# A gated cross-attention kernel: order of the visits, place of a sigmoid, and the softmax's small steps

## The chip, the cores and the metric

The kernel runs on one core of a Trainium2 chip. The metric is the device time of one execution in microseconds (us), the median of several runs. All data is fp32. The engines of the core are TensorE (PE in the profile; its weight loads are listed apart as PEld), VectorE (DVE), ScalarE (ACT), GpSimd (POOL) and SyncE (SP), which issues most DMAs.

## The reference

```python
# x: 8 x 1024 x 1024, ctx: 8 x 64 x 512
memory_proj = einsum('bme,de->bmd', ctx, W_mem)            # W_mem 1024 x 512
scores = einsum('bnd,bmd->bnm', x, memory_proj) / sqrt(1024)
attn = softmax(scores, axis=-1)                             # over 64 rows of memory
memory_context = einsum('bnm,bmd->bnd', attn, memory_proj)
gate = sigmoid(einsum('bnf,df->bnd', concat([x, memory_context]), W_gate) + b_gate)
fused = x + gate * memory_context
out = fused * rsqrt(mean(fused**2) + 1e-6) * norm_w
```

The gate's second half is not computed from `memory_context`: the kernel multiplies `memory_proj` with that half of `W_gate` once, so that each row's gate gets `attn` times the result, as its context gets `attn` times `memory_proj`.

## The kernel before, in words

The 8192 rows of `x` are taken in 16 passes (`q`) of 512 rows, two passes per batch. In each pass the product of x (512 x 1024) with the first half of `W_gate` is made by a fast matrix multiplication on two levels: seven outer products (`ORDER` = 1, 6, 7, 5, 4, 2, 3, line 633), each of them seven inner products of 128 x 256 x 256, where the operands are sums and differences made beforehand by VectorE and GpSimd. Some outer products' results go into several blocks of the gate.

`outer_product(q, o)` (line 889) issues one outer product. Its inner products are, in order: R11 into the bank `af`, whose result ScalarE copies at once into `u` (L910, "the first copy"); one into the bank `b` (`kB`); one into the bank `c` (`kC`); two into the bank `ed`; and two more into `af`, the sixth and seventh. VectorE's additions `u<-u,kB`, `u<-u,kC` and `u<-u,ed` follow their products. `pre` (GpSimd), `fin_ed` and `fin_af` (VectorE) add the results to the gate's blocks (tiles `gate`); all of these show as L96, the helper `tt`, and all matmuls as L93, the helper `mm`.

Two outer products of a pass, o=5 and o=2, are "held": their banks `af` and `ed` are not read at the end but kept until the next outer product, o=4 or o=3. There, behind the third inner product, stand the "visits": `visit` (line 830) multiplies the 64 rows of memory of this batch with the attention weights of one row block of 128 rows and one half of the columns, once into a context bank `pc`, once, added, into the gate's bank (`af` or `ed`). There are four visits, two for the held block (`f`) and two for the block of this outer product (`o`), in the order o first row, f first, f second, o second. The held block's contexts go into the banks `b` and `c`, from which VectorE's additions of `kB` and `kC` read just before. Then come the held block's additions `fin_af` and `fin_ed` and its gating: `gate` (line 882) issues the sigmoid on ScalarE (L695) and puts the multiplication with the context (`gated`, line 689) into a later slot. The own block's second row is gated after the fifth inner product, its first row after the seventh.

Order on an engine is program order. The program is written by slots: every inner product of 128 x 256 is one slot, a pass has 49, and `at(slot, fn)` or `mid((q, o, part), fn)` puts a step ahead of that slot's product or beside the visits of an outer product. `plan(q)` (line 636) places a pass's steps. Those of the softmax: the scores of the next pass are made by TensorE behind the visits of o=3 (`scores`, line 400), in pass q from 1 on into the two banks `af` and `ed` that the held block has just left, in pass 0 into `b` and `c` at slot 7; `turn_scores` in slot 1 turns them and takes the maxima over 32 columns, `softmax_max` in slot 8 copies the maxima between halves of the partitions, `softmax_exp` in slot 9 takes the larger, scales it by -1/32 on ScalarE (L447), takes the exponentials with their sums (L450) and copies the sums across, `softmax_scale` in slot 15 adds and inverts the sums (L464) and scales (L466), `turn_attn` in slot 19 turns the result. `transpose_x` turns the next pass's rows in 32 x 32 blocks on VectorE (L353), in slots 20 to 38 and, for two of the eight pieces, beside the visits of o=3.

The last pass (q=15) has no next pass; its additions of the residual, its squares and its norm are placed one by one (`last_gated`, `last_root`, `last_norm`).

Of the kernel before, what the change touches and what calls it, by code (L numbers as in the profile page):

```python
# [9 lines left out]
AF = mybir.ActivationFunctionType  # L10
ALU = mybir.AluOpType
# [4 lines left out]
P = 128  # L16
# [4 lines left out]
def tile_gated_cross_attention_rmsnorm(  # L21
# [42 lines left out]
    nc = tc.nc  # L64
# [11 lines left out]
    SCALE = 1.0 / float(D) ** 0.5  # L76
    Q4 = D // 4
    B32 = 32
# [6 lines left out]
    small = ctx.enter_context(tc.tile_pool(name="small", bufs=1))  # L85
# [4 lines left out]
    pin = tc.keep_in_program_order  # L90

    def mm(o, lhsT, rhs, start, stop):
        pin(nc.tensor.matmul(o, lhsT, rhs, start=start, stop=stop, skip_group_check=True))  # L93

    def tt(eng, o, a, b, op):
        pin(eng.tensor_tensor(o, a, b, op))  # L96
# [4 lines left out]
    def t4k(pool, shape, tag, name):  # L101
        return pool.tile(shape, F32, tag=tag, name=name)
# [31 lines left out]
    for k in range(KD):  # L134
        t = t4k(*((gpool, [P, D], "gate") if k < 7 else (apool, [P, D], "s4")), f"w2_{k}")
# [42 lines left out]
    eps_sb = const.tile([P, 1], F32, name="eps_sb")  # L178
# [161 lines left out]
    sTs, attnTs, scs, mxs, dens, mps, mgs = {}, {}, {}, {}, {}, {}, {}  # L340
# [90 lines left out]
        mx = mxs[q] = t4k(small, [P, 2, 8], "mx", f"mx{q}")  # L431
        pin(nc.vector.tensor_reduce(mx[:, 0], sc, AX.X, ALU.max))

    def other_half(o, i):

        for g in range(4):
            pin(nc.scalar.copy(o[g * B32 : (g + 1) * B32], i[(g ^ 1) * B32 : ((g ^ 1) + 1) * B32]))

    def softmax_max(q):
        mx = mxs[q]  # L440
        other_half(mx[:, 1], mx[:, 0])

    def softmax_exp(q):
        sc, mx = scs[q], mxs.pop(q)
        den = dens[q] = t4k(small, [P, 2, 8], "den", f"den{q}")
        tt(nc.vector, mx[:, 0], mx[:, 0], mx[:, 1], ALU.max)
        pin(nc.scalar.activation(mx[:, 0], mx[:, 0], AF.Copy, scale=-SCALE))  # L447
        for n in range(8):
            pin(
                nc.scalar.activation(  # L450
                    sc[:, n],
                    sc[:, n],
                    AF.Exp,
                    bias=mx[:, 0, n : n + 1],
                    scale=SCALE,
                    accum_out=den[:, 0, n : n + 1],
                )
            )
        other_half(den[:, 1], den[:, 0])

    def softmax_scale(q):
        sc, den = scs[q], dens.pop(q)
        tt(nc.vector, den[:, 0], den[:, 0], den[:, 1], ALU.add)
        pin(nc.vector.reciprocal(den[:, 0], den[:, 0]))  # L464
        for n in range(8):
            pin(nc.scalar.activation(sc[:, n], sc[:, n], AF.Copy, scale=den[:, 0, n : n + 1]))  # L466

# [158 lines left out]
    def at(slot, fn, *args):  # L626
        due.setdefault(slot, []).append(lambda: fn(*args))

    def mid(key, fn, *args):
        beside.setdefault(key, []).append(lambda: fn(*args))  # L630
# [5 lines left out]
    def plan(q):  # L636
        t0 = SLOTS * q
        nxt = q + 1 < NQ
        for i, o in enumerate(ORDER):
            for part, t in ((0, 1), (1, 2)):  # L640
                if i + 1 < len(ORDER):
                    at(t0 + 7 * i + t, inner_s, q, ORDER[i + 1], part)
                elif nxt:
                    at(t0 + 7 * i + t, inner_s, q + 1, ORDER[0], part)
        if q == 0:
            at(t0 + 7, scores, q)
            at(t0 + 8, add_scores, q)
        at(t0 + (3 if q else 7), outer_s, q, 3)
        at(t0 + (11 if q else 22), outer_s, q, 4)
        when = (9, 10, 11, 16, 19, 23) if q == 0 else (1, 8, 9, 15, 19, 23)  # L650
        steps = turn_scores, softmax_max, softmax_exp, softmax_scale, turn_attn, attn_difference
        for t, fn in zip(when, steps):
            at(t0 + t, fn, q)
        if not nxt:
            at(t0 + 12, load_last)
            return
        at(t0 + 2, load_xq, q + 1)
        for i, t, half in (
            (20, 0, 0), (21, 1, 0), (23, 2, 0), (25, 3, 0), (37, 2, 1), (38, 3, 1)
        ):  # L660
            at(t0 + i, transpose_x, q + 1, t, half)
        mid((q, 3, 0), transpose_x, q + 1, 0, 1)
        mid((q, 3, 1), transpose_x, q + 1, 1, 1)
        mid((q, 3), scores, q + 1)
        at(t0 + 46, add_scores, q + 1)
        mid((q, 3), outer_s, q + 1, 1)
        mid((q, 3), outer_s, q + 1, 2)
        if (q + 1) % QPB == 0:
            at(t0 + 10, load_mp, (q + 1) // QPB)
            at(t0 + 49, load_mg, (q + 1) // QPB)  # L670
        if q == 0:
            at(t0 + 8, add_bias, mgs[0][M:P, :])
            at(t0 + 20, add_bias, mgd[1, M:, :])
# [8 lines left out]
    slot = 0  # L682
# [116 lines left out]
            )  # L799
        load(out[b, n0 : n0 + P, cols], g)  # L800

    def sqrt_table():

        t = t4k(small, [P, 1], "warm", "warm")
        pin(nc.scalar.activation(t, eps_sb, AF.Sqrt))  # L805

    def blocks(q, row, r, h):

        t = 2 * row + r
        if (q, t) not in O:  # L810
            O[q, t] = t4k(gpool, [P, D], "gate", f"gate{q}_{t}")
        return O[q, t].rearrange("p (n c) -> p n c", c=C)[:, 2 * h : 2 * h + 2]
# [17 lines left out]
    def visit(q, o, r, pc, k):  # L830

        row, h, g = EXT[o]
        at_, mg = attnTs[q], mgs[q // QPB]
        second = o in SECOND
        cols = slice(h * H, (h + 1) * H)
        for t in TOKENS:
            mm(pc[t, :], at_[0:M, 2 * row + r, t], mg[0:M, cols], True, True)
        if second and r == 0:
            for n, left in ((0, g + r), (1, NEG[o])):
                part = mg[M:P, h * H + n * C : h * H + (n + 1) * C]  # L840
                for t in TOKENS:
                    mm(k[t, n], at_[M:P, upper(left), t], part, False, True)
        else:
            whole = k.rearrange("p n c -> p (n c)")
            for t in TOKENS:
                mm(whole[t, :], at_[M:P, upper(g + r), t], mg[M:P, cols], second, True)
# [42 lines left out]
    def outer_product(q, o):  # L889
# [4 lines left out]
        nxt = q + 1 < NQ  # L894
        af = bank(f"af{sets}", [P, 2, C], f"af{q}_{o}")
# [24 lines left out]
        if second:  # L920
            f = SECOND[o]
            faf, fed, fu3, fu4 = held.pop((q, f))
            frow, fh, _ = EXT[f]
            fp = [bank(t, [P, H], f"pc{q}_{f}_{r}") for r, t in enumerate("bc")]
            pcs = [ps_ctx.tile([P, H], F32, tag="ctx", name=f"pc{q}_{o}_{r}") for r in range(2)]
            visit(q, o, 0, pcs[0], af)
            visit(q, f, 0, fp[0], faf)
            visit(q, f, 1, fp[1], fed)
            visit(q, o, 1, pcs[1], ed)
        for fn in beside.pop((q, o, 0), ()):  # L930
            fn()
# [24 lines left out]
        if second:  # L956
            row, h, _ = EXT[o]
# [5 lines left out]
        if not first:  # L963
            fin_af(q, o, af, u4)
        if second:
            if o == 4 and not nxt:
                at(slot + 1, gate, q, 2 * row, h, pcs[0], 1)
            else:
                gate(q, 2 * row, h, pcs[0], 1)
        if second and not nxt:  # L970
            c, d = 2 * row, 2 * row + 1
            if o == 3:
                sqrt_table()
            when = (3, 4, 4, None, 10, 11) if o == 4 else (0, 2, 2, 2, 3, 3)
            if o == 4:
                for h_ in range(2):
                    mid((q, 3, 0), last_weigh, c, h_)
            at(slot + when[0], last_root, d)
            at(slot + when[1], last_root, c)
            for w_, (t, h_) in zip(when[2:], ((d, 0), (d, 1), (c, 0), (c, 1))):  # L980
                if w_ is None:
                    mid((q, 3, 0), last_norm, t, h_)
                else:
                    at(slot + w_, last_norm, t, h_)
        elif second:

            c, d = 2 * row, 2 * row + 1
            for t in (d, c):
                at(slot + 5, residual, q, t)
            if row == 0:  # L990
                when = (22, 23, -1, None, 33, -2) if q + 2 < NQ else (17, 18, 20, 22, 24, -1)
            else:
                when = (17, 18, 22, 24, 29, 31)
            at(slot + when[0], square, q, c)
            at(slot + when[1], square, q, d)
            for w_, (t, h_) in zip(when[2:], ((c, 0), (c, 1), (d, 0), (d, 1))):
                if w_ is None:
                    mid((q + 1, 4), norm, q, t, h_)
                elif w_ < 0:
                    mid((q + 1, 4, 0) if w_ == -1 else (q + 1, 3), norm, q, t, h_)  # L1000
                else:
                    at(slot + w_, norm, q, t, h_)
# [6 lines left out]
    while due:  # L1009
        slot = min(due)  # L1010
# [27 lines left out]
```

## Time and profile before

| | before |
|---|---|
| median of 3 runs | 952.65 us (952.65 to 952.77) |
| profiled execution | 951.76 us, of which span 950.0 us |
| mean granted TensorE clock | 0.996 |
| TensorE busy | 937.4 us, 99% of the span |
| VectorE busy | 818.1 us, 86% |
| GpSimd busy | 727.4 us, 77% |
| ScalarE busy | 414.0 us, 44% |

The share of TensorE is close to the whole span, so a change counts where TensorE's stream has a gap, or behind its last product. Timelines give the start of a group of like instructions in us from the span's start, how long the group lasted, the engine, the line, the operation with the program's names (out<-in), the number of instructions, and, in brackets, how long the engine was idle before and what ended that. A matmul of 128 x 256 in fp32 shows as two records, so an inner product shows as x4. In the rows of weight loads and of matmuls an idle time is counted on the queue of that kind.

### The profile page before, as it was taken

Reading aid. Unit: us, or ns where it says so; the run is one execution under the profiler, and the core shown is the slowest. Engines: PE = TensorE matmul, PEld = TensorE weight load, DVE = VectorE, ACT = ScalarE, POOL = GpSimd, SP = SyncE. Lnnn points to the kernel's source line nnn. Section 1 sums busy time; section 2 is a strip of 40 time slices with the busy share of each in tenths; the row PEclk is TensorE's granted clock in tenths of the full one; section 3 lists DMA queues with packets and bytes.
Section 4 is the critical chain, followed back from the end, with each engine's and each line's share of the span. In section 5 each row is a group of like instructions: output and inputs, shape, how many; then the busy total and the mean of one; then the engine's idle time right before and its main releaser. Section 6 shows DMA issues by size and latency. Waiting matters only on the chain. (4 is left out here: it accounts for less than half of the span.)

```text
span 950.0 us, 15819 instructions
## 1 busy us (share of the span) xinstructions
PE 937.4 (99%) x5560; PEld 730.6 (77%) x5560; DVE 818.1 (86%) x1274; ACT 414.0 (44%) x1086; POOL 727.4 (77%) x812
## 2 busy tenths in 40 slices
PE   9999999999999999999999999999999999999995
PEld 8546778787877778787877778787877778687873
DVE  6989788888988888888988888888988888888877
ACT  3000436273544527263543627263543627263555
POOL 5998878688687878678686868778686868778684
PEclk9999999999999999999999999999999999999998
DMA  9956664481919365491918366390918466390632
GB/s 377 285 146 163 104 123 110 110 179 44 212 45 181 93 141 131 97 192 34 220 48 166 101 135 144 85 204 27 213 61 158 110 133 145 76 213 25 150 138 90
DMA packets 70928, 128.44 MB, mean 135 GB/s; under 512 B 12352, under 2 KB 49216, under 8 KB 70592
## 3 DMA queue, kind: packets, MB, share of 16 engines
q1 hardware_dynamic: 61664, 93.86, 37.5%
q0 software_dynamic: 9184, 33.56, 19.4%
q8 instruction: 45, 0.74, 0.3%
q14 instruction: 35, 0.29, 0.1%
HBM read 87.56 MB, written 41.68 MB: 136 GB/s over the span
## 5 line engine op out<-in xcount | busy, mean ns | idle before, releaser
L96 POOL TENSOR_TENSOR gate<-gate,u 128x512 f32<-128x512 f32 (+1 forms) x224 | 237.6, 1072 | 162.2 <-DVE u L96 137.6
L695 ACT ACTIVATE gate<-gate 128x512 f32<-128x512 f32 x128 | 80.7, 630 | 263.8 <-DVE gate L96 263.8
L353 DVE STREAM_TRANSPOSE a<-xq 128x512 f32<-128x512 f32 x128 | 141.3, 1107 | 3.7 <-POOL it L96 3.7
L96 POOL TENSOR_TENSOR l<-a 128x256 f32<-128x256 f32 x128 | 116.4, 909 | 24.2 <-DVE a L96 22.7
L724 DVE SCALAR_TENSOR_TENSOR gate<-gate,ss,nw_sb 128x512 f32<-128x512 f32 x120 | 123.9, 1032 | 1.1
L93 PE MATMUL pc<-mg,attnT 64*64 64x512 f32 x512 | 117.0, 596 | 0.3 <-DVE u L96 0.3
L93 PE MATMUL ed<-it,l 128*128 128x256 f32 x448 | 115.0, 379 | 0.0
L93 PE MATMUL kB<-it,l 128*128 128x256 f32 x448 | 115.0, 379 | 0.0
L96 DVE TENSOR_TENSOR gate<-gate,pc 128x512 f32<-128x512 f32 x128 | 86.1, 682 | 31.7 <-ACT gate L695 31.7
L93 PE MATMUL af<-w,a 128*128 128x256 f32 x384 | 98.5, 379 | 0.0
L96 DVE TENSOR_TENSOR gate<-gate,af 128x512 f32<-128x512 f32 (+1 forms) x128 | 77.1, 612 | 20.0 <-PE af L93 11.6
L93 PEld LDWEIGHTS ed<-it,l 128*128 128x128 f32 x448 | 85.1, 190 | 11.6
L93 PEld LDWEIGHTS kB<-it,l 128*128 128x128 f32 x448 | 85.1, 190 | 11.6
L96 DVE TENSOR_TENSOR gate<-gate,ed 128x512 f32<-128x512 f32 x112 | 76.3, 681 | 17.1 <-POOL gate L96 13.5
L910 ACT COPY u<-af 128x256 f32<-128x256 f32 x112 | 40.9, 365 | 105.8 <-PE af L93 100.2
L93 PEld LDWEIGHTS af<-w,a 128*128 128x128 f32 x384 | 73.0, 190 | 10.4 <-issue 0.5
L96 POOL TENSOR_TENSOR l<-s 128x256 f32<-128x256 f32 x96 | 78.1, 813 | 3.0 <-PE af L93 3.0
L93 PEld LDWEIGHTS pc<-mg,attnT 64*64 64x64 f32 x512 | 33.0, 132 | 49.8 <-issue 44.8
L93 PE MATMUL ed<-it,a 128*128 128x256 f32 x256 | 67.4, 386 | 0.0
L96 DVE TENSOR_TENSOR u<-u,kB 128x256 f32<-128x256 f32 x112 | 45.6, 407 | 24.6 <-PE kB L93 21.0
L93 PE MATMUL af<-w,l 128*128 128x256 f32 x256 | 66.4, 382 | 0.1
L93 PE MATMUL af<-t,s 128*128 128x256 f32 x256 | 65.8, 379 | 0.0
(149 smaller groups left out, 2100.1 us busy)
## 6 DMA issues: line engine op xcount, KB each, us to landing
xq<-in_x SPq DMA_DIRECT2D x64, 512.0 KB, 10.3
gate<-in_x POOLq DMA_DIRECT2D x60, 512.0 KB, 8.1
out<-gate SPq DMA_DIRECT2D x60, 512.0 KB, 2.9
w<-in_w_gate_t SPq DMA_DIRECT2D x8, 512.0 KB, 10.2
w<-in_w_gate_t SPq DMA_DIRECT2D x2, 2048.0 KB, 16.9
mg<-mgd SPq DMA_DIRECT2D x16, 256.0 KB, 5.0
wm<-in_w_mem_t SPq DMA_DIRECT2D x4, 512.0 KB, 6.0
mpd<-mpT SPq DMA_DIRECT2D x4, 512.0 KB, 8.3
```

The costliest lines, as they stand in the source:

```text
L93: pin(nc.tensor.matmul(o, lhsT, rhs, start=start, stop=stop, skip_group_check=True))
L96: pin(eng.tensor_tensor(o, a, b, op))
L353: nc.vector.transpose(A[key][:, :, r * P : (r + 1) * P], chunks(xq[q][:, 4 * t : 4 * t + 4, :], KD)[:, half * KH : (half + 1) * KH],)
L695: pin(nc.scalar.activation(g, g, AF.Sigmoid))
L724: nc.vector.scalar_tensor_tensor(g[:, cols], g[:, cols], rstd[:, t % 2 : t % 2 + 1], nw_sb[:, cols], ALU.mult, ALU.mult,)
L910: pin(nc.scalar.copy(p1, af[:, 0]))
```

## The change

- Visits: the held block's two rows come first, then the two rows of the own block.
- Sigmoid: in all passes but the last, the gate of the own block's first row is issued one slot later for both o=4 and o=3: its sigmoid stands behind the next outer product's first copy, its multiplication another slot later. (In the last pass o=4 did so already, and o=3 stays as it is.)
- Maxima: the copies between halves multiply by -1/32 as they copy; VectorE then scales the own half and takes the smaller in one instruction, and ScalarE's scaling (L447) goes.
- exp's table: behind these copies, in slot 8, a one-element exp is issued, so that the table is loaded there.
- Sums: their addition and inversion become a step of their own, `softmax_sum`, in slot 13 (15 in pass 0); the scaling stays in slot 15 (16 in pass 0).
- `transpose_x` of piece (0, 1) goes from beside the visits of o=3 to slot 42, ahead of o=3's first product.

```diff
-    def other_half(o, i):
+    def other_half(o, i, scale):
         for g in range(4):
-            pin(nc.scalar.copy(o[g * B32 : (g + 1) * B32], i[(g ^ 1) * B32 : ((g ^ 1) + 1) * B32]))
+            pin(
+                nc.scalar.activation(
+                    o[g * B32 : (g + 1) * B32],
+                    i[(g ^ 1) * B32 : ((g ^ 1) + 1) * B32],
+                    AF.Copy,
+                    scale=scale,
+                )
+            )
+    def table(func):
+        t = t4k(small, [P, 1], "warm", "warm")
+        pin(nc.scalar.activation(t, eps_sb, func))
     def softmax_max(q):
         mx = mxs[q]
-        other_half(mx[:, 1], mx[:, 0])
+        other_half(mx[:, 1], mx[:, 0], -SCALE)
+        table(AF.Exp)
     def softmax_exp(q):
...
-        tt(nc.vector, mx[:, 0], mx[:, 0], mx[:, 1], ALU.max)
-        pin(nc.scalar.activation(mx[:, 0], mx[:, 0], AF.Copy, scale=-SCALE))
+        pin(nc.vector.scalar_tensor_tensor(mx[:, 0], mx[:, 0], -SCALE, mx[:, 1], ALU.mult, ALU.min))
...
-        other_half(den[:, 1], den[:, 0])
+        other_half(den[:, 1], den[:, 0], 1.0)
+    def softmax_sum(q):
+        den = dens[q]
+        tt(nc.vector, den[:, 0], den[:, 0], den[:, 1], ALU.add)
+        pin(nc.vector.reciprocal(den[:, 0], den[:, 0]))
     def softmax_scale(q):
         sc, den = scs[q], dens.pop(q)
-        tt(nc.vector, den[:, 0], den[:, 0], den[:, 1], ALU.add)
-        pin(nc.vector.reciprocal(den[:, 0], den[:, 0]))
...
-        when = (9, 10, 11, 16, 19, 23) if q == 0 else (1, 8, 9, 15, 19, 23)
-        steps = turn_scores, softmax_max, softmax_exp, softmax_scale, turn_attn, attn_difference
+        when = (9, 10, 11, 15, 16, 19, 23) if q == 0 else (1, 8, 9, 13, 15, 19, 23)
+        steps = (
+            turn_scores,
+            softmax_max,
+            softmax_exp,
+            softmax_sum,
+            softmax_scale,
+            turn_attn,
+            attn_difference,
+        )
...
-            (20, 0, 0), (21, 1, 0), (23, 2, 0), (25, 3, 0), (37, 2, 1), (38, 3, 1)
+            (20, 0, 0), (21, 1, 0), (23, 2, 0), (25, 3, 0), (37, 2, 1), (38, 3, 1), (42, 0, 1)
...
-        mid((q, 3, 0), transpose_x, q + 1, 0, 1)
         mid((q, 3, 1), transpose_x, q + 1, 1, 1)
...
-            visit(q, o, 0, pcs[0], af)
             visit(q, f, 0, fp[0], faf)
             visit(q, f, 1, fp[1], fed)
+            visit(q, o, 0, pcs[0], af)
             visit(q, o, 1, pcs[1], ed)
...
-            if o == 4 and not nxt:
+            if nxt:
+                at(slot + 1, gate, q, 2 * row, h, pcs[0], 1)
+            elif o == 4:
                 at(slot + 1, gate, q, 2 * row, h, pcs[0], 1)
             else:
                 gate(q, 2 * row, h, pcs[0], 1)
...
             if o == 3:
-                sqrt_table()
+                table(AF.Sqrt)
```

More of the change, by code (lines that the diff above doesn't have):

```diff
@@ L800, in last_norm @@
         load(out[b, n0 : n0 + P, cols], g)
-    def sqrt_table():
-        t = t4k(small, [P, 1], "warm", "warm")
-        pin(nc.scalar.activation(t, eps_sb, AF.Sqrt))
     def blocks(q, row, r, h):
```

## The prediction

> **What bounds the kernel now.** I read the page first, then the waits of TensorE's weight loads (PEld), because a matmul's end is modelled and its own waits hide stalls, and then timelines of pass 7 and of the last pass. Passes are the 16 groups of 512 rows; o=5, 4, 2, 3 are outer products; "visits" are the attention matmuls (`pc`, with `af` and `ed` beside them) ahead of the fourth product of o=4 and o=3.
>
> ```profile
> span 950.0 us, 15819 instructions
> PE 937.4 (99%) x5560; PEld 730.6 (77%) x5560; DVE 818.1 (86%) x1274; ACT 414.0 (44%) x1086; POOL 727.4 (77%) x812
> ```
>
> TensorE is the bound: it has work for 99% of the span. The changed lines add no matmul and take none away, so only three things can move the time: a stall of TensorE inside its stream, the tail behind its last product, and new stalls. Weight loads run ahead of matmuls, so their idle time shows where TensorE was held:
>
> ```profile
> PEld psT_af L93 <- DVE gate L96: 4.1, 15, 0.3
> PEld af L93 <- POOL l L96: 3.7, 10, 0.7
> PEld af L93 <- issue: 1.3, 4, 0.4
> ```
>
> Two places come back pass after pass: the scores (`psT`, 15 times) and a product into `af` (10 times). Pass 7 shows the second, VectorE, then ScalarE, then TensorE:
>
> ```profile
> 495.83 0.68 DVE L96 TENSOR_TENSOR gate<-gate,af 128x512 f32<-128x512 f32 x1
> 497.20 0.69 DVE L96 TENSOR_TENSOR gate<-gate,pc 128x512 f32<-128x512 f32 x1 [0.70 <-ACT gate L695]
> ```
> ```profile
> 496.54 0.63 ACT L695 ACTIVATE gate<-gate 128x512 f32<-128x512 f32 x1 [1.35 <-DVE gate L96]
> 497.08 0.35 ACT L910 COPY u<-af 128x256 f32<-128x256 f32 x1
> ```
> ```profile
> 495.70 1.03 PE L93 MATMUL ed<-it,a 128*128 128x256 f32 x4
> 496.57 1.03 PE L93 MATMUL ed<-it,l 128*128 128x256 f32 x4
> 497.58 1.10 PE L93 MATMUL af<-w,l 128*128 128x256 f32 x4
> ```
>
> Products follow each other at 0.87 (495.70 to 496.57); the sixth product of o=2 comes 1.01 after the fifth, and its four matmuls take 1.10 where the others take 1.03: 0.21 lost. It writes the bank from which the first copy (L910) reads. That copy ended at 497.43, 0.15 before, because it stood behind the last sigmoid of o=4, which waited for VectorE until 496.51.
>
> **The change part by part.**
>
> *Sigmoid behind the copy.* The copy no longer queues behind that sigmoid. The product that it reads ends two products before 495.70, near 494.0, so even behind one other 0.63 sigmoid it ends well over 1 us before 497.43. Ten weight-load idles of 3.7 stand under the POOL name; the longest, 0.7, belongs to the last pass (below). Nine at pass 7's 0.21 make 1.9, and one more, in pass 0, stands under "issue" (longest 0.4): I take 0.3. **Term 1: -2.2.** The price of the edit is that the gating multiply comes one product later, behind the addition of `kB` and a transposition. Its `pc` bank isn't wanted until the visits of the next outer product but one, and ahead of it the 0.70 in which VectorE waited for the sigmoid goes.
>
> *Held block first.* Pass 7's rows around the visits of o=3, VectorE and TensorE:
>
> ```profile
> 500.48 0.39 DVE L96 TENSOR_TENSOR u<-u,ed 128x256 f32<-128x256 f32 x1
> 501.37 0.42 DVE L96 TENSOR_TENSOR u<-u,kB 128x256 f32<-128x256 f32 x1 [0.51 <-PE kB L93]
> 502.17 0.42 DVE L96 TENSOR_TENSOR u<-u,kC 128x256 f32<-128x256 f32 x1 [0.37 <-PE kC L93]
> 502.51 1.11 DVE L353 STREAM_TRANSPOSE a<-xq 128x512 f32<-128x512 f32 x1
> 504.14 0.69 DVE L96 TENSOR_TENSOR gate<-gate,af 128x512 f32<-128x512 f32 x1 [0.53 <-PE af L93]
> 504.93 0.69 DVE L96 TENSOR_TENSOR gate<-gate,ed 128x512 f32<-128x512 f32 x1
> ```
> ```profile
> 502.06 0.65 PE L93 MATMUL pc<-mg,attnT 64*64 64x512 f32 x2
> ```
> ```profile
> 505.55 0.38 PE L93 MATMUL psT_af<-a,mpb 64*64 64x256 f32 x2
> 505.68 0.43 PE L93 MATMUL psT_ed<-a,mpb 64*64 64x256 f32 x2
> ```
> ```profile
> 508.78 0.38 PE L93 MATMUL psT_af<-a,mpb 64*64 64x256 f32 x2
> 508.97 0.38 PE L93 MATMUL psT_ed<-a,mpb 64*64 64x256 f32 x2
> 509.28 0.48 PE L93 MATMUL ed<-it,s 128*128 128x256 f32 x1
> ```
>
> Four visits take 3.49 (502.06 to 505.55), 0.87 each. The scores of the next pass write the two banks of the held block, and these are free only after its two additions, the second of which ends at 505.62. So `psT_ed` starts at 505.68, and the lag stays: the last `psT_ed` comes 0.19 behind its twin, and the next product 0.31 behind that. Pass 0 writes its scores to other banks and has no lag, 0.02:
>
> ```profile
> 88.99 0.38 PE L93 MATMUL psT_b<-a,mpb 64*64 64x256 f32 x2
> 89.01 0.38 PE L93 MATMUL psT_c<-a,mpb 64*64 64x256 f32 x2
> ```
>
> With the held block visited first, its second addition can start one visit, 0.87, sooner and end at 504.75, 0.80 before the scores. The lag falls from 0.19 to 0.02 in 15 passes. **Term 2: -2.5.** Next late is nothing: the other operands, the transposed rows, are wanted half-way through the scores, and their last transposition moves forward with the additions.
>
> What the old order covered: the held block's matmuls write the banks of `kB` and `kC`, so they wait for the additions that read these. In front, the first needs the `kB` addition, done at 501.79 against 502.06: 0.27 spare. The second visit, at 502.93, needs the `kC` addition, done at 502.59: 0.34 spare. So no cost while VectorE is no later than today. No row has the new order of matmul shapes; by the 3.49 against four visits at a product's 0.87 it could cost or gain 0.03 a group, 1.0 over 32 groups; I take 0, since the shapes stay the same.
>
> *Transposition to slot 42.* It goes from 502.51, where it stood ahead of the held additions, to between the `u<-u,ed` addition of o=2 (ends 500.87) and the `kB` addition (501.37). At 1.11 it doesn't fit there today: the queue behind it is the `kB` addition, and now TensorE's first visit. But VectorE gets there sooner: from 497.20 to 500.87 it works without a break, and the 0.70 ahead of that is gone, so 500.17 at the latest, and the transposition ends by 501.28. The `kB` product is 0.21 sooner too, so its addition starts near 501.2 and the first visit is due at 501.85; 501.28 + 0.42 = 501.70. Cost 0 with 0.15 to spare, or more, since o=4's held additions come sooner as well.
>
> *Maxima, exp's table, sum.* Pass 8:
>
> ```profile
> 522.03 0.21 ACT L447 ACTIVATE mx<-mx 128x8 f32<-128x8 f32 x1 [0.88 <-DVE mx L96]
> 522.26 1.28 ACT L450 ACT_TABLE_LOAD   x1
> 526.13 0.81 ACT L437 COPY den<-den 32x8 f32<-32x8 f32 x4
> ```
> ```profile
> 525.67 0.67 DVE L96 TENSOR_TENSOR gate<-gate,ed 128x512 f32<-128x512 f32 x1
> ```
>
> The copies of the maxima end at 521.15; the load now starts there, beside VectorE's step, and with the one-element exp (0.2) the exponentials start near 522.65 instead of 523.55. The sums' copies end 0.9 sooner, at 526.04, before VectorE is through with the 525.67 addition behind which the moved sum now stands (526.34). So the sum holds nobody, and ScalarE can scale sooner. The loads stay as many: no square root or sigmoid lies between the new exp and the exponentials. All of this is beside TensorE: 0 in the middle of the kernel.
>
> *The last pass.* ScalarE waits 1.53 there for the reciprocals, then has two squares and a table load, and the first copy of o=5 comes late:
>
> ```profile
> 904.27 1.80 ACT L466 ACTIVATE sc<-sc,den 128x32 f32<-128x32 f32 x8 [1.53 <-DVE den L464]
> ```
> ```profile
> 910.66 0.36 ACT L910 COPY u<-af 128x256 f32<-128x256 f32 x1
> ```
> ```profile
> 911.17 1.10 PE L93 MATMUL af<-t,l 128*128 128x256 f32 x4 [0.30 <-ACT u L910]
> ```
>
> Here the waits name the copy, again 0.15 after its end. The earlier sum takes away most of the 1.53, so this stall goes: the 0.7 of its weight load less the 0.15 that this idle has over the loss, 0.54. Then the tail:
>
> ```profile
> 917.74 0.69 DVE L96 TENSOR_TENSOR gate<-gate,af 128x512 f32<-128x512 f32 x1 [0.86 <-PE af L93]
> ```
> ```profile
> 932.95 0.65 PE L93 MATMUL pc<-mg,attnT 64*64 64x512 f32 x2 [0.32 <-DVE u L96]
> ```
> ```profile
> 939.03 0.38 PE L93 MATMUL af<-w,s 128*128 128x256 f32 x1
> ```
> ```profile
> 939.88 0.69 DVE L96 TENSOR_TENSOR gate<-gate,af 128x512 f32<-128x512 f32 x1 [0.24 <-POOL gate L96]
> ```
>
> From 917.74 VectorE is late, not TensorE. It starts there 0.86 + 0.54 = 1.40 sooner. The visit that waits 0.32 for VectorE at 932.95 moves to the front: wanted 0.87 + 0.54 = 1.41 sooner, with VectorE 1.40 sooner, so that wait stays. The last gate addition (939.88) then waits for TensorE's last product, 939.41 - 0.54 = 938.87, and the rest hangs on it unchanged. **Term 3: -1.0.** If VectorE gains nothing, the front visit waits 0.9 more and the term is +0.4; if it gains all its 1.4, -1.4. One more bound:
>
> ```profile
> 921.07 1.72 DVE L96 TENSOR_TENSOR gate<-gate,xl 128x512 f32<-128x512 f32 x1
> ```
> ```profile
> 920.97 1.27 POOL L96 TENSOR_TENSOR gate<-gate,u 128x512 f32<-128x512 f32 x1
> ```
>
> This residual addition takes 1.72 where VectorE's like-sized ones above take 0.69, with GpSimd at work: 1.03 that the shifted times can lose or spare. The Trainium skill, "GPSIMD Engine Reference", Specifications, says the two share their SBUF interface and contend when a VectorE instruction has two SBUF inputs; the trace agrees, and by that rule the residual additions collide and those reading PSUM don't. In this sum one collision fewer changes nothing, since TensorE's last product decides (938.87); one more eats the 0.42 that VectorE has over it (1.40 less 0.98) and 0.6 of the term, which would be -0.4. I take none.
>
> Sum: -2.2 - 2.5 - 1.0 = -5.7 on the profiled 951.76 (span 950.0 and 1.8 around it). The median, 952.65, lies 0.9 higher; I take the difference over (the three runs before lie within 0.12): **947.0**.
>
> **The rivals.** *The weight loads' name is right:* GpSimd's `l`, not the copy, holds the sixth product. Then term 1 is gone: 949.2. Against it: the copy ends 0.15 before the product here and in the last pass. *The scores' lag stays,* say because a norm or the transposition gets in ahead of the second addition: 949.5. Against it: only the order of visits holds that addition (504.83 to 504.93 idle). *Slower: the transposition at slot 42.* If VectorE ends the o=2 addition no sooner than today, 500.87, the transposition ends at 501.98 and the `kB` addition at 502.40; the first visit, due at 501.85, waits 0.57, 15 times 8.6, against 5.7: 955.5. It costs from 500.3 on and decides from about 0.2 before today's 500.87. For it: the cover is truly taken away and the spare is 0.15. Against: the 0.70.
>
> **How the numbers follow.** About 0.2%, 1.9 us, can be told from no change. Forecast 0.60; the wrong cause 0.10; the lag stays 0.10; a partly late transposition that eats most of the gain 0.12 (within 1.9 of before); fully late 0.08. Faster 0.80, same 0.12, slower 0.08. The range goes from 945.9 (shapes' 1.0 gained) to 949.8 (either lost term, and 0.3 more).
>
> **What would show it.** Right: the sixth product of o=2 follows at 0.87; `psT_ed` starts within 0.02 of `psT_af`; the `af` and `psT` rows leave the weight loads' waits; the first `pc` of each group follows the third product as today; ScalarE's wait ahead of the scaling is gone. Wrong: a `pc <- DVE u` wait 15 times or more.

## The result and the profile after

The changed kernel takes 946.85 us (median of 6 runs, 946.26 to 947.96) against 952.65 (6 runs, 951.50 to 952.83): ratio 0.9943, 95% interval 0.9931 to 0.9956, that is 4.2 to 6.6 us less. The forecast was 947.0.

The page of the profiled execution (947.65 us):

```profile
span 945.9 us, 15834 instructions
PE 932.7 (99%) x5560; PEld 726.0 (77%) x5560; DVE 801.4 (85%) x1274; ACT 419.0 (44%) x1086; POOL 734.3 (78%) x812
```

TensorE is still the bound. VectorE does as many instructions in 16.7 us less: hold on to that number, it comes back below.

This span is 4.1 shorter than before, not 5.7. Part of it is the start. GpSimd's first copy, which waits for a load of weights, first in the kernel before, then in the changed one:

```profile
6.92 1.11 POOL L285 COPY pm_it<-wm 128x512 f32<-128x512 f32 x1 [5.61 <-DMA wm<-in_w_mem_t]
```
```profile
7.79 1.09 POOL L285 COPY pm_it<-wm 128x512 f32<-128x512 f32 x1 [6.48 <-DMA wm<-in_w_mem_t]
```

The load came 0.87 later in this execution. Ahead of it nothing is changed, and of the other eleven kernels below three had such a late load too (7.69 to 7.97). The load isn't the only thing that moves the start: in one kernel below (no_sigmoid) the load is early, 6.88, and the first scores still come at 86.39. So I compare from the first scores of pass 0 (85.71 before, 86.57 after) to the end of the span, and call that the main part: 864.3 before, 859.3 after, 5.0 less. It splits, by the starts of the visits, as follows:

| piece | before | after | difference |
|---|---|---|---|
| o=4's to o=3's visits, passes 1 to 14, sum over the shortest, 15.883 each | 1.86 | 0.00 | -1.86 |
| the same, pass 0 | 16.18 | 16.41 | +0.23 |
| o=3's visits to the next pass's o=4, 14 times | 37.63 | 37.47 | -2.3 |
| the same, into the last pass | 38.17 | 37.47 | -0.70 |
| last pass, o=4's to o=3's visits | 15.88 | 16.13 | +0.24 |
| last pass, o=3's visits to the end | 18.45 | 17.88 | -0.57 |

The waits of the weight loads now:

```profile
PEld pc L93 <- issue: 23.6, 96, 0.3
PEld pc L93 <- DVE u L96: 23.3, 64, 0.9
PEld ed L93 <- issue: 19.6, 32, 0.8
PEld psT_af L93 <- issue: 8.1, 30, 0.3
```

The rows `af <- POOL l` and `psT_af <- DVE gate` are gone. The row `pc <- DVE u` looks like the slower rival come true, 64 times. It isn't: all idle time ahead of `pc` loads was 46.2 before (44.8 under "issue", 1.1 and 0.3 under VectorE) and is 46.9 now. The same pauses have got another name, because the last semaphore to arrive is now that of the addition; only two of the 64 are waits that hold TensorE, the longest, 0.9 in pass 0, and one in the last pass (both shown below).

Pass 7 at o=2, VectorE, ScalarE and TensorE:

```profile
493.24 0.68 DVE L96 TENSOR_TENSOR gate<-gate,af 128x512 f32<-128x512 f32 x1
494.23 0.42 DVE L96 TENSOR_TENSOR u<-u,kB 128x256 f32<-128x256 f32 x1 [0.30 <-PE kB L93]
494.56 1.10 DVE L353 STREAM_TRANSPOSE a<-xq 128x512 f32<-128x512 f32 x1
495.61 0.63 DVE L96 TENSOR_TENSOR gate<-gate,pc 128x512 f32<-128x512 f32 x1
```
```profile
493.35 0.37 ACT L927 COPY u<-af 128x256 f32<-128x256 f32 x1 [0.74 <-POOL l L96]
493.96 0.63 ACT L717 ACTIVATE gate<-gate 128x512 f32<-128x512 f32 x1 [0.24 <-DVE gate L96]
```
```profile
495.68 1.03 PE L93 MATMUL ed<-it,l 128*128 128x256 f32 x4
496.55 0.81 PE L93 MATMUL af<-w,l 128*128 128x256 f32 x3
```

The first copy (L927 here) stands ahead of the sigmoid (L717) and ends at 493.72, and the sixth product follows the fifth at 0.87. But see also the first row: VectorE is through with o=4's last addition 1.76 before the fifth product starts (493.92 against 495.68); before, it was 496.51 against 496.57. Even behind the sigmoid, the copy would now have ended near 495. Which edit did it is a question for the experiments.

The scores of pass 8, and the held block's additions ahead of them:

```profile
504.44 0.38 PE L93 MATMUL psT_af<-a,mpb 64*64 64x256 f32 x2
504.46 0.38 PE L93 MATMUL psT_ed<-a,mpb 64*64 64x256 f32 x2
```
```profile
507.68 0.38 PE L93 MATMUL psT_af<-a,mpb 64*64 64x256 f32 x2
507.70 0.38 PE L93 MATMUL psT_ed<-a,mpb 64*64 64x256 f32 x2
508.01 0.48 PE L93 MATMUL ed<-it,s 128*128 128x256 f32 x1
```
```profile
502.18 0.69 DVE L96 TENSOR_TENSOR gate<-gate,af 128x512 f32<-128x512 f32 x1 [0.70 <-PE af L93]
502.97 0.69 DVE L96 TENSOR_TENSOR gate<-gate,ed 128x512 f32<-128x512 f32 x1
```

The second addition ends at 503.66, 0.8 before the scores, and the lag is 0.02.

Two new waits stand at the front visits, one in pass 0, one in the last pass (VectorE of pass 0, then TensorE of both):

```profile
125.74 0.38 DVE L96 TENSOR_TENSOR u<-u,ed 128x256 f32<-128x256 f32 x1
126.03 1.12 DVE L353 STREAM_TRANSPOSE a<-xq 128x512 f32<-128x512 f32 x1
127.07 0.38 DVE L96 TENSOR_TENSOR u<-u,kB 128x256 f32<-128x256 f32 x1
```
```profile
127.51 0.65 PE L93 MATMUL pc<-mg,attnT 64*64 64x512 f32 x2 [0.45 <-DVE u L96]
```
```profile
928.00 0.65 PE L93 MATMUL pc<-mg,attnT 64*64 64x512 f32 x2 [0.17 <-DVE u L96]
```

In pass 0 the moved transposition holds the addition of `kB` and so the visit: by the pieces above 0.53. The last pass's costs 0.24.

### The profile page after: what moved, and what is told of

It reads as the page before. It is cut to its first block, busy times and chain, and to the rows that moved or that the text cites. A ratio compares the mean times of both kernels' runs of the same rounds, so it can differ in the third digit from the quotient of the medians.

```text
span 945.9 us, 15834 instructions
## 1 busy us (share of the span) xinstructions
PE 932.7 (99%) x5560; PEld 726.0 (77%) x5560; DVE 801.4 (85%) x1274; ACT 419.0 (44%) x1086; POOL 734.3 (78%) x812
## 4 chain that ended last, share of the span: by engine, by line
PE 96%; DVE 2%; DMA 1%; ACT 1%; issue 0%; POOL 0%; SPq 0%; DVEq 0%
PE af L93 32%; PE ed L93 21%; PE pc L93 10%; PE kC L93 10%; PE kB L93 10%; PE pg L93 5%; PE psT_af L93 5%; PE pm L93 2%; DVE gate L96 1%; DMA wm<-in_w_mem_t 1%; PE psT_ed L93 0%; DVE gate L820 0%; PE psT_b L93 0%; ACT junk L787 0%; DVE u L96 0%
## 5 line engine op out<-in xcount | busy, mean ns | idle before, releaser
L96 POOL TENSOR_TENSOR gate<-gate,u 128x512 f32<-128x512 f32 (+1 forms) x224 | 244.5, 1103 | 154.1 <-DVE u L96 151.3
L717 ACT ACTIVATE gate<-gate 128x512 f32<-128x512 f32 x128 | 80.6, 630 | 184.0 <-DVE gate L96 182.5
L96 POOL TENSOR_TENSOR l<-a 128x256 f32<-128x256 f32 x128 | 112.2, 877 | 17.0 <-PE af L93 15.8
L927 ACT COPY u<-af 128x256 f32<-128x256 f32 x112 | 41.5, 371 | 165.6 <-PE af L93 155.5
L746 DVE SCALAR_TENSOR_TENSOR gate<-gate,ss,nw_sb 128x512 f32<-128x512 f32 x120 | 110.1, 917 | 1.1
L96 POOL TENSOR_TENSOR l<-s 128x256 f32<-128x256 f32 x96 | 84.7, 882 | 3.0 <-PE af L93 3.0
L93 PE MATMUL af<-mg,attnT 64*64 64x256 f32 (+1 forms) x384 | 67.4, 456 | 0.0
```

Source lines behind the costliest of these rows:

```text
L717: pin(nc.scalar.activation(g, g, AF.Sigmoid))
L746: nc.vector.scalar_tensor_tensor(g[:, cols], g[:, cols], rstd[:, t % 2 : t % 2 + 1], nw_sb[:, cols], ALU.mult, ALU.mult,)
L927: pin(nc.scalar.copy(p1, af[:, 0]))
```

## Experiments

Theory at the start: each edit has its own term, the sigmoid's place that of the ten stalls (passes 0 and 3 to 11), the order of visits that of the scores' lag. Rivals: GpSimd's tile holds the sixth product; or VectorE's lateness is a common cause that one edit alone could mend. The measured numbers:

| kernel | median (its runs of before) | ratio, 95% interval | first scores | main part |
|---|---|---|---|---|
| before | 952.65 | | 85.71 | 864.3 |
| changed | 946.85 (952.65) | 0.9931 to 0.9956 | 86.57 | 859.3 |
| order_only | 947.66 (953.31) | 0.9924 to 0.9954 | 85.72 | 859.3 |
| sigmoid_only | 949.60 (953.31) | 0.9948 to 0.9974 | 85.76 | 861.7 |
| slot42_only | 952.80 (953.31) | 0.9991 to 1.0010 | 85.70 | 864.4 |
| softmax_only | 952.87 (953.31) | 0.9983 to 1.0002 | 86.10 | 865.0 |
| order_slot42 | 947.70 (953.19) | 0.9922 to 0.9958 | 86.65 | 859.5 |
| no_sigmoid | 947.16 (953.19) | 0.9921 to 0.9952 | 86.39 | 859.9 |
| no_order | 948.74 (953.19) | 0.9936 to 0.9967 | 85.65 | 861.3 |
| no_slot42 | 946.33 (953.19) | 0.9916 to 0.9948 | 85.74 | 858.8 |
| no_pre4 | 950.35 (953.68) | 0.9953 to 0.9979 | 86.75 | 861.8 |
| order_sigmoid | 947.19 (953.68) | 0.9917 to 0.9947 | 85.92 | 859.0 |
| last_own_first | 947.20 (953.68) | 0.9918 to 0.9951 | 86.48 | 858.8 |

The medians carry the start's spread; differences of under 1 us between the kernels are read from the main part. It is that of one traced execution for each kernel, so it has no interval; what speaks for it is that a piece without a wait comes out within 0.01 from pass to pass and from kernel to kernel (15.88 from o=4's to o=3's visits).

**order_only** (on the kernel before):

```diff
-            visit(q, o, 0, pcs[0], af)
             visit(q, f, 0, fp[0], faf)
             visit(q, f, 1, fp[1], fed)
+            visit(q, o, 0, pcs[0], af)
```

> The kernel before with the held block's visits first and nothing else. Main part (from the first scores of pass 0 to the end of the span; 864.3 before, 859.3 after). Theory (each edit has its own term): the lag of the scores goes in 15 passes, -2.5, and the ten stalls of o=2's sixth product and the one of the last pass stay: 861.8, and the tail 0.3 to 0.9 less: 861 to 861.5. Rival (the common cause is VectorE's lateness, which the order alone mends): the ten stalls go too, another -2.2: 859 to 859.5.

The order alone gives the whole gain: 859.3. The lag is gone, and of the ten stalls one is left, pass 0's 0.28. (Small new waits of 0.14 and 0.10 stand at the front visits of o=4 in passes 3 and 15.) The theory of one term per edit falls; the rival stands. Why does VectorE come sooner by so much? Its norm in o=4 of pass 7 and GpSimd's addition beside it, first in the kernel before:

```profile
490.65 1.75 DVE L724 SCALAR_TENSOR_TENSOR gate<-gate,ss,nw_sb 128x512 f32<-128x512 f32 x1
```
```profile
490.59 1.26 POOL L96 TENSOR_TENSOR gate<-gate,u 128x512 f32<-128x512 f32 x1
```

and in order_only:

```profile
487.97 0.91 DVE L724 SCALAR_TENSOR_TENSOR gate<-gate,ss,nw_sb 128x512 f32<-128x512 f32 x1
```
```profile
488.30 1.72 POOL L96 TENSOR_TENSOR gate<-gate,u 128x512 f32<-128x512 f32 x1
```

Before, GpSimd began 0.06 ahead and VectorE's norm took 1.75. Now the norm begins 0.33 ahead, takes 0.91, and GpSimd's addition takes 1.72 instead of 1.26. The one that starts second is the one that is stretched. (The norm's 0.91 is over the 0.75 that it takes alone because GpSimd's addition ahead of that one, `l<-a,l` at 487.61 for 0.72, had begun before it.) It holds beyond this pair: over all thirteen traces there are 169 cases in which a norm began up to 1.0 behind a GpSimd addition to `gate` of 128x512 that met no other norm, and there the addition always took 1.26 to 1.31 and the norm ended 1.80 to 1.85 after the addition's start; in the 511 such cases in which the norm began first, by 0.16 to 0.50, the addition took 1.55 to 1.74. The order moves VectorE 0.74 forward at the held additions (1.34 behind the first visit, against 2.08) and 0.86 at the norm (3.84 against 4.70), GpSimd's addition only 0.46 (4.17 against 4.63), and that turns the collision round: from there on VectorE is 1.7 ahead.

**no_pre4** tests that collision by itself. On the kernel before, GpSimd's first addition of o=4 is left out, so that the gate lacks one term in that block:

```diff
-        pre(q, o, u3, None)
+        if o != 4:
+            pre(q, o, u3, None)
```

> The kernel before without GpSimd's first addition of o=4 (the gate then lacks one term in that block): it takes away the instruction beside which VectorE's norm took 1.75 us. Main part 864.3 before. Theory (that collision makes VectorE late and so the copy): the norm takes 0.8, VectorE reaches o=4's last addition 1.0 sooner, the ten stalls go, the scores' lag stays: 862.1. Rival (VectorE is late from its wait for the second visit alone): norm as long as before or stalls as before, 864 and more.

```profile
490.90 0.75 DVE L724 SCALAR_TENSOR_TENSOR gate<-gate,ss,nw_sb 128x512 f32<-128x512 f32 x1
```

The norm begins where it did, 4.70 behind the first visit, and takes 0.75; from there on VectorE is 1.0 sooner, and the stalls go but for pass 0's: 861.8. (That is under the expectation because the stall into the last pass shrinks as well, 38.17 to 37.75, and the end, 18.45 to 18.28.) So 1.0 us of a stretched norm, some five us upstream, was enough to make the stalls of passes 3 to 11.

**sigmoid_only** (on the kernel before):

```diff
-            if o == 4 and not nxt:
+            if nxt or o == 4:
                 at(slot + 1, gate, q, 2 * row, h, pcs[0], 1)
```

> The kernel before with only the sigmoid of the own block's first row behind the next outer product's first copy. Theory (the copy in ScalarE's queue holds the sixth product of o=2): all ten stalls go, -2.2, main part 862.1. Rival (GpSimd's l tile holds it, as the weight loads' waits name it): 864.3, ten stalls as before.

All ten stalls go, and 0.4 of the last pass's: 861.7. By itself this doesn't clear GpSimd's tile, because in this kernel VectorE's norm in pass 7 takes 1.27 instead of 1.75, and GpSimd's `l` comes 0.3 sooner with it. Two things in the traces do. In all ten stalls before, the sixth product starts 0.145 behind the copy's end. And pass 0 has GpSimd's tile late without a stall; GpSimd, the copy and the product there, first in the kernel before, then GpSimd and the product in the changed one:

```profile
120.30 0.73 POOL L96 TENSOR_TENSOR l<-l,s 128x256 f32<-128x256 f32 x1
121.44 0.35 ACT L910 COPY u<-af 128x256 f32<-128x256 f32 x1
121.93 1.10 PE L93 MATMUL af<-w,l 128*128 128x256 f32 x4
```
```profile
121.25 0.73 POOL L96 TENSOR_TENSOR l<-l,s 128x256 f32<-128x256 f32 x1
122.57 1.03 PE L93 MATMUL af<-w,l 128*128 128x256 f32 x4
```

Before, this `l` was done 0.90 ahead of the product, and the product was late; after, it is done only 0.59 ahead (each of the four `l` of that outer product stands 0.3 later against the product), and the product follows the fifth at 0.87 (121.71 to 122.57). What moved the other way is the copy, done 1.8 ahead. So the copy held the sixth product, not GpSimd's tile. **no_sigmoid** is the reverse, the changed kernel with that line as before:

> The changed kernel with the sigmoid back in its old place. Theory now (VectorE's lateness is the common cause, and the order mends it): the ten stalls stay away, main part 859.3 to 859.6, pass 0 perhaps 0.3 more. Rival (term 1 of the prediction belongs to the sigmoid's place): the ten stalls are back, 861.4.

859.9: the stalls of passes 3 to 11 stay away; pass 0's is there, again 0.145 behind the copy. Pass 0 makes the 0.6 over the changed kernel, most of it (0.49 ahead of o=4's visits) not foreseen, and its cause isn't shown. Each edit alone mends the nine stalls, and both together mend them once; pass 0's goes with the sigmoid's place alone.

**slot42_only** (on the kernel before) and **order_slot42** (with the order as well):

```diff
-            (20, 0, 0), (21, 1, 0), (23, 2, 0), (25, 3, 0), (37, 2, 1), (38, 3, 1)
+            (20, 0, 0), (21, 1, 0), (23, 2, 0), (25, 3, 0), (37, 2, 1), (38, 3, 1), (42, 0, 1)
...
-        mid((q, 3, 0), transpose_x, q + 1, 0, 1)
```

> The kernel before with only the transposition moved to slot 42. Theory (the own block's visit in front covers VectorE's kB addition): the kB addition ends up to 0.4 us behind the first visit in most passes, but no visit waits: main part 864.3. Rival (something else in front wants VectorE): longer by 0.3 us a pass, 868.

> The kernel before with the held block's visits first and the transposition in slot 42, without the sigmoid's and the softmax's edits. Main part (859.3 with the order alone). Theory (the order frees VectorE by 1.7 us in o=4, so the transposition has room): 859.3 to 859.9, waits of the first visit only in passes 0 and 15, 0.5 each. Rival (the slower case of the prediction: the transposition pushes the kB addition behind the front visit): a wait of 0.3 to 0.6 in each of passes 0 to 14, 864 to 868.

864.4 and 859.5. With the old order the own visit covers the late addition: in slot42_only the addition of `kB` ends 0.07 to 0.14 behind that visit's start in twelve of the 15 passes, where it ended 0.27 ahead of it before. A visit that waits for this addition starts 0.06 behind its end (as in the changed kernel's pass 0), so in front it would have waited 0.1 to 0.2 in those passes; that is an estimate, no run has it. With the new order, of o=3's visits only those of pass 0 (16.35) and the last pass (16.44, in which nothing is transposed) wait. The slower rival needs VectorE as late as before, and the order takes that lateness away, so it shows in pass 0 alone.

**softmax_only** (on the kernel before, all softmax edits of the change):

> The kernel before with only the softmax's edits (maxima scaled in their copies, exp's table in slot 8, the sum in its own step). Theory: the stall in the last pass goes, -0.54, and nothing else: main part 863.4 to 863.8, the ten stalls and the scores' lag as before. Rival (ScalarE's earlier scaling frees the middle of each pass): the ten stalls shrink as well, 861.6.

865.0. The stall in the last pass went (38.17 to 37.63 into it), the ten stalls stayed about as they were, but pass 0 lost 1.1 (o=4's to o=3's visits 17.26 against 16.18), which no theory had. TensorE waited there twice:

```profile
118.98 1.10 PE L93 MATMUL kB<-it,l 128*128 128x256 f32 x4 [0.16 <-DVE gate L96]
119.91 1.03 PE L93 MATMUL kC<-w,l 128*128 128x256 f32 x4
120.78 1.03 PE L93 MATMUL ed<-it,a 128*128 128x256 f32 x4
121.64 1.03 PE L93 MATMUL ed<-it,l 128*128 128x256 f32 x4
123.41 1.10 PE L93 MATMUL af<-w,l 128*128 128x256 f32 x4 [0.74 <-ACT u L928]
```

VectorE is later there, because two of its operand sums met GpSimd's additions the other way round than before. VectorE, then GpSimd, first in the kernel before, then in softmax_only:

```profile
114.94 0.69 DVE L96 TENSOR_TENSOR it<-w 128x512 f32<-128x512 f32 x1
115.66 1.10 DVE L96 TENSOR_TENSOR it<-w,it 128x512 f32<-128x512 f32 x1
```
```profile
114.97 1.24 POOL L96 TENSOR_TENSOR l<-a,l 128x256 f32<-128x256 f32 x1
116.17 1.72 POOL L96 TENSOR_TENSOR gate<-gate,u 128x512 f32<-128x512 f32 x1
```
```profile
115.33 1.22 DVE L96 TENSOR_TENSOR it<-w 128x512 f32<-128x512 f32 x1
116.59 1.64 DVE L96 TENSOR_TENSOR it<-w,it 128x512 f32<-128x512 f32 x1
```
```profile
115.28 0.72 POOL L96 TENSOR_TENSOR l<-a,l 128x256 f32<-128x256 f32 x1
115.97 1.72 POOL L96 TENSOR_TENSOR gate<-gate,u 128x512 f32<-128x512 f32 x1
```

Counted from o=4's first visit (110.24 and 110.63), VectorE's sum begins at 4.70 in both. GpSimd's `l` begins at 4.73 before and at 4.65 here, just ahead of the sum instead of just behind it, and the two sums end 1.1 later. The 0.08 goes back to GpSimd's additions for the turned attention weights (`attnT`), which stand that much sooner.

**no_order** (the changed kernel with the visits as before):

> The changed kernel with the visits in the old order. Theory now: the sigmoid's place alone keeps the ten stalls away, but the scores' lag is back in 15 passes, +2.5, and the own block's visit covers the waits of passes 0 and 15, -0.8: main part 861.0 to 862. Rival (the order's gain lies elsewhere than in the lag): psT_ed within 0.02 of psT_af, 859.3 or less.

861.3, no wait in any piece from o=4's to o=3's visits (15.88 in all 16 passes), and 37.63 from each o=3 to the next pass's o=4: in the stream the lag, and nothing else, is what the sigmoid and the softmax can't mend.

**no_slot42** (the changed kernel with the transposition back):

```diff
-            (20, 0, 0), (21, 1, 0), (23, 2, 0), (25, 3, 0), (37, 2, 1), (38, 3, 1), (42, 0, 1)
+            (20, 0, 0), (21, 1, 0), (23, 2, 0), (25, 3, 0), (37, 2, 1), (38, 3, 1)
...
+        mid((q, 3, 0), transpose_x, q + 1, 0, 1)
```

> The changed kernel with the transposition back beside the visits of o=3. Theory (the move costs its 0.5 in pass 0, where three more VectorE additions stand ahead of it, and gains nothing elsewhere): main part 858.8, scores without lag. Rival (beside the visits it holds the held block's second addition past the start of the scores): the lag is back in part, 860 to 861.5.

858.8, as expected; pass 0's visits stand 15.88 apart. This one, by 0.5 of the main part, is better than the changed kernel: the move of the transposition costs and brings nothing.

**order_sigmoid** (the kernel before with these two edits):

> The kernel before with the new order of visits and the sigmoid behind the copy, and nothing else. Theory (the softmax's edits are worth only their part of the last pass): main part 859.0, that is the 859.3 of the order alone less pass 0's stall of 0.3, with 0.2 to 0.3 in the last pass over the best so far (858.8). Rival (the softmax's edits free VectorE in each pass): 860 or more.

859.0. The softmax's three edits and their new small instructions are worth 0.2 beside them, against no_slot42's 858.8: the two small waits at the front visits of o=4 in passes 3 and 15 go (0.14 and 0.11), and of the last pass's front wait 0.33, but the end behind it takes 0.36 more (17.89 against 17.53).

**last_own_first** (no_slot42, and in the last pass's o=3 the own first row's visit in front):

```diff
+            if not nxt and o == 3:
+                visit(q, o, 0, pcs[0], af)
             visit(q, f, 0, fp[0], faf)
             visit(q, f, 1, fp[1], fed)
-            visit(q, o, 0, pcs[0], af)
+            if nxt or o == 4:
+                visit(q, o, 0, pcs[0], af)
```

> The changed kernel with the transposition back beside the visits, and, in the last pass's o=3, the own block's first row visited first. Theory (the front wait of 0.25 goes, but the held block's gating comes 0.87 later and the tail with it): main part 858.8, as without that edit. Rival (the tail has slack): 858.5.

858.8, as without: the front wait of 0.25 goes (15.88), and the end comes 0.26 later behind it (18.15 against 17.89). No wait is left between o=4's and o=3's visits in any pass, and the tail takes what the visits give.

## Why the prediction was right, step by step

*Term 1, -2.2 for the ten stalls.* Size right: 2.16 was there to gain, -1.86 in passes 1 to 14, and in pass 0 its 0.30. The mechanism in its last link is shown too: the copy in ScalarE's queue. The credit was wrong in part. The working took VectorE's lateness at 496.51 as given and gave the whole term to the sigmoid's place; order_only and no_sigmoid show that the order alone makes VectorE 1.7 sooner and ends nine of the ten stalls. The step "fin additions of o=4 come sooner as well" stood in the working only as a bit of spare. Because both edits mend the same stalls, the sum, which counted them once, came out right; that the credit didn't matter to the number is luck.

*Term 2, -2.5 for the scores' lag.* Right in place, size and cause: 0.16 in each of 15 passes, 0.02 left, back in no_order.

*Transposition at slot 42, 0.* Right in passes 1 to 14, and with more room than the 0.15 worked out. Wrong in pass 0, +0.53: the working was that of pass 7, and in pass 0 three sums of weights stand on VectorE in between. The slower rival was a true mechanism, near the price that it was given (0.57 a pass), in one pass of fifteen; slot42_only points to a smaller price in the others.

*Term 3, -1.0 in the last pass.* The stall went (-0.54), and softmax_only shows that the earlier sum does it, but here too the credit is shared: the order alone takes all of it but 0.10, the sigmoid's place all but 0.11. The front wait was put at today's 0.3 and is 0.24. The last gate addition, which the working had wait for TensorE's last product, does so:

```profile
935.78 0.69 DVE L96 TENSOR_TENSOR gate<-gate,af 128x512 f32<-128x512 f32 x1 [1.08 <-PE af L93]
```

The sum of the last pass is -0.87. That the wait is now 1.08 long shows VectorE, no longer late, with time to spare.

*The softmax.* Exponentials 0.9 sooner, reckoned back from the visits of pass 8: 16.1 ahead before, 17.1 after. ScalarE's wait ahead of the scaling is gone. Nothing of it reaches TensorE in the middle, as forecast.

*The collision of VectorE and GpSimd* was a bound in term 3 alone. It was the lever behind the nine stalls, as no_pre4 shows, though not behind the lag, which stayed there (37.63). Of VectorE's 16.7 us less of busy time in the changed kernel 13.8 are in the norms (123.9 before, 110.1 after). The Trainium skill, "GPSIMD Engine Reference", Specifications, names that contention for VectorE instructions with two SBUF inputs; the norm is one, and the trace agrees (1.75 beside GpSimd's addition, 0.75 without it).

*What would show it wrong* was badly put: "a `pc <- DVE u` wait 15 times or more" came true in name, 64 times, without the time.

Sum of the pieces: -1.63, -2.46 and -0.87 make -5.0 in the main part, against -5.7; the difference is pass 0's 0.53, 0.13 of the last pass and small remainders. The medians differ by 5.8, 0.8 more, which is within the spread of the start: the traced execution before is 0.9 under its kernel's median, the one after 0.8 over. So that 946.85 lies so close to 947.0 is in part luck.

## What to carry to other kernels

When a stall ends at a short instruction in a queue, ask for the instruction that made the one ahead of it late, and on back: two edits that mend one chain count once, whichever of them gets the credit. Work a moved step through in the first and last passes as well as in a middle one, since they carry extra work. And judge a wait by its time summed over all names, not by the name that a row gives it.

## What the runs showed of the hardware that was not expected

Of a norm of VectorE and an addition of GpSimd that meet, both of 128x512 with all inputs in SBUF, the one that started second was stretched: VectorE's norm took 1.75 when it began 0.06 behind GpSimd's addition (1.26), 0.91 when it began 0.33 ahead (GpSimd then 1.72), and 0.75 with that addition left out. So a shift of a few tenths moved about a microsecond from one engine to the other, and in pass 0 of softmax_only a shift of 0.08 was enough.

The copy that waits for the first load of weights began at 6.92 and at 7.79 with nothing changed ahead of it, and the first scores came 0.86 apart with it.
